# A transformer block on one core: the order of the first chunk's work, of the first-key subtraction and of the second group's normalization

## The chip, the core and the metric

One core of a Trainium2 chip runs the whole kernel. A core has TensorE (PE: matmuls and transposes, results in PSUM), VectorE (DVE), ScalarE (ACT) and GpSimd (POOL) for elementwise work, and SyncE (SP), whose queue issues all the DMAs here. Each engine runs its own queue in order; semaphores tie the queues together. The metric is the device time of one execution in microseconds (us). Before the change it is 1096.91 us, the median of 3 runs (1096.4 to 1098.2).

## The reference

Two sequences of 2048 rows with 256 channels pass a layer norm and latent attention with 16 heads, and then a layer norm and a gated FFN with 768 hidden channels; both are added to their input. Everything is fp32. Cut to what matters:

```
h    = layernorm(x)                                   # [2, 2048, 256]
kv_c = rmsnorm(h @ W_kv) * g_kv                       # 64 channels
q_c  = h @ W_q                                        # 128 channels
k    = concat(kv_c @ W_kdec, rope(h @ W_krope))       # per head 16 + 32
q    = concat(q_c @ W_qdec, rope(q_c @ W_qrope))
v    = kv_c @ W_vdec                                  # per head 16
attn = softmax(causal(q k^T / sqrt(48))) v
x    = x + attn @ W_o
h    = layernorm(x)
out  = x + (silu(h @ w_gate^T) * (h @ w_up^T)) @ w_down^T
```

## The kernel before, in words

The rows are cut into 8 chunks of 512, four for each sequence (b, g). The program has three stages, one after the other, and a fourth that is skipped with these inputs.

**Projections.** Each chunk's x is loaded (L64). `measure` takes the moments (`bn_stats` L78 and `bn_aggr` L80 on DVE, then the inverse root as an addition and a power on POOL, L69 and L70). `norm` subtracts and scales (L86, DVE). `turn` transposes the eight 128x128 blocks on PE (L97) into one PSUM tile, which ACT copies out in one instruction (L98). `compressed` makes kv (L252) and q (L255), with ACT copies, a square on ACT, a sum on DVE (L264) and an inverse root on POOL. `kv_norm` (L272, ACT) scales kv, `kv_turn` (L279) transposes it. Four rope projections, k_0, q_0, k_1, q_1 (L298 and L301), each fill a two-bank PSUM tile, which DVE reads twice to multiply it with the cosine and sine tables (L306); POOL subtracts and adds the products (L308, L309), and SP writes the result to DRAM (L311). The content projections (L319, copied by ACT L322, written at L325 and L328) and v (L335, L342) follow. The PSUM tiles come from a pool with four buffers, so a projection waits until the reader of the fourth one before it is done. The tile of cosine products has three buffers, each free when its write to DRAM has landed; the tile of sine products has two.

The loop over chunks interleaves three chunks: while chunk i is projected, chunk i + 1 is transposed and compressed, and the moments of chunk i + 2 are taken. The raw weights are loaded in front, behind the first x: w_kr, w_kv, w_q, then the first 512 columns of the tables, x of chunk 1, w_qh and the rest. `rope_columns` (L205) reorders w_kr's columns on ACT. `staged` (L168) puts raw weights into the buffers of the cosine products or of the content projections.

**Attention.** There are 32 steps (b, u, g): sequence, group of four heads, chunk of queries. A step goes through the key chunks c = 0 to g; the scores (L535, PE) go through exp (L540, ACT), on the diagonal through a mask (L547, POOL), and into the sums with v (L561, PE). No maximum is subtracted; in its place, `from_first` subtracts the sequence's first key from all keys, since that leaves the softmax as it is: on DVE, two copies of the first key (L140, only for g = 0) and two subtractions (L141) of 48x1024 for each tile of keys. Each step adds one key tile. In the projections, from the fifth chunk on, `load_first` takes from a list: the loads of the first four key tiles, of the first two query tiles, and then the four `from_first`, one entry at each of four places in a chunk. In attention, step i subtracts for step i + 3 after its fourth score block. In the last three steps the work for the FFN's groups 0 and 1 begins: `projected` (L459) and `added` (L465) for both, `measured`, `normed` and `normalized` (L499 to L501) for group 0.

**FFN.** For each of the 8 groups of 512 rows, six blocks of 128 hidden channels: gate and up on PE (L692; inputs and hidden values are split into a rounded part and a rest, `hi` and `lo`), silu on ACT (L695), the product on DVE (L699), its rest on POOL (L704). Between the blocks stand the next groups' pieces: `measured` of group i + 1 behind block 0; `finished` (the down projection of group i - 1, L720), `normed` of group i + 1, `inverted` (the reciprocal of the sums, L436), `projected` and `added` of group i + 2 behind block 1; `normalized` of group i + 1 behind block 3. `ps_o`, the transposes `tp_f` and `gu` share three PSUM buffers.

**What sets the order.** Every stage stands in a `manual_schedule` over all five engines. Where an instruction ends up in its engine's queue is decided there, and it isn't always the place that it has in the source.

Of the kernel before, what the change touches and what calls it, by code (L numbers as in the profile page):

```python
# [9 lines left out]
FP = mybir.dt.float32  # L10
# [3 lines left out]
ALU = mybir.AluOpType  # L14
# [4 lines left out]
P = 128  # L19
B, T, C = 2, 2048, 256  # L20
NH, HD, RD = 16, 16, 32
KVR, QR = 64, 128
HID = 768
CH = 512
NC = T // CH
NT = CH // P
# [14 lines left out]
def block_kernel(ctx: ExitStack, tc: tile.TileContext, x, w_kv, g_kv, w_kc, w_v, w_q, w_qh, w_kr, w_o,  # L41
                 w_gate_t, w_up_t, w_down_t, cos_t, sin_t, out):
    nc = tc.nc
# [6 lines left out]
    small = ctx.enter_context(tc.tile_pool(name="small", bufs=3))  # L50
# [11 lines left out]
    def load_x(pool, b, g, **kw):  # L62
        t = pool.tile([P, NT, C], FP, tag="x", name=f"x_{b}_{g}", **kw)
        nc.sync.dma_start(out=t, in_=x[b, g * CH:(g + 1) * CH, :].rearrange("(t p) d -> p t d", p=P))  # L64
        return t

    def inverse_sqrt(dst, src, eps):

        nc.gpsimd.tensor_scalar_add(dst, src, eps)  # L69
        nc.gpsimd.tensor_tensor(dst, dst, neg_half, ALU.pow)  # L70

    def moments(src, name):

        stats = small.tile([P, NT, 6], FP, tag="stats", name=f"stats_{name}")
        mv = small.tile([P, NT, 2], FP, tag="mv", name=f"mv_{name}")
        rstd = small.tile([P, NT], FP, tag="rstd", name=f"rstd_{name}")
        for t in range(NT):
            nc.vector.bn_stats(out=stats[:, t, :], in_=src[:, t, :])  # L78
        for t in range(NT):
            nc.vector.bn_aggr(out=mv[:, t, :], in_=stats[:, t, :])  # L80
        inverse_sqrt(rstd, mv[:, :, 1], LN_EPS)
        return mv, rstd

    def scaled(dst, src, mv, rstd):
        for t in range(NT):
            nc.vector.tensor_scalar(dst[:, t, :], src[:, t, :], mv[:, t, 0:1], rstd[:, t:t + 1],  # L86
                                    ALU.subtract, ALU.mult)

# [60 lines left out]
    with ExitStack() as actx:  # L149
# [5 lines left out]
        def two(name):  # L155
            return ps_two.tile([P, 2, CH], FP, tag="two", name=name)

        actx.enter_context(tc.manual_schedule(engines=order))
        xt = {(0, 0): load_x(prep, 0, 0, bufs=3)}

        def weight(src, shape, name, split=None):
            w = acst.tile(shape, FP, tag=name, name=name)
            nc.sync.dma_start(out=w, in_=src.rearrange("(c p) f -> p c f", p=P) if split else src)
            return w

        def staged(src, shape, name):
            w = rope.tile(shape, FP, tag="tcos" if shape[0] == P else "done", bufs=3 if shape[0] == P else 2, name=name)
            nc.sync.dma_start(out=w, in_=src)  # L168
            return w

        w_kr_raw = [staged(w_kr[d * P:(d + 1) * P, :], [P, NH * 64], f"w_kr_raw_{d}") for d in range(2)]
        w_kv_sb = weight(w_kv, [P, 2, KVR], "w_kv_sb", True)
        w_q_sb = weight(w_q, [P, 2, QR], "w_q_sb", True)

        tables = []
        for name, src in (("cos", cos_t[:RD // 2]), ("sin", sin_t[RD // 2:])):
# [23 lines left out]
        def rope_columns(w, raw):  # L200

            to = w.rearrange("p (e s h r) -> p s e h r", e=2, s=2, h=8)
            of = raw.rearrange("p (e h s r) -> p s e h r", e=2, h=8, s=4)
            for s in range(2):
                nc.scalar.copy(to[:, s], of[:, s])  # L205
# [8 lines left out]

        w_kc_sb = acst.tile([P, P], FP, tag="w_kc", name="w_kc_sb")
        w_kr_sb = acst.tile([P, 2, NH * RD], FP, tag="w_kr", name="w_kr_sb")
        for d in range(2):
            rope_columns(w_kr_sb[:, d, :], w_kr_raw[d])

        def columns():  # L220
            rope_columns(w_qr_sb, w_qh_raw)
# [129 lines left out]
        def job(i, k):  # L351
            if i < len(chunks):
                chains[i][k]()

        for k in (measure, norm, turn):
            job(0, k)
        job(1, measure)

        first_loads = ([(load_k, step) for step in steps[:NC]] + [(load_q, step) for step in steps[:AHEAD]]
                       + [(from_first, step) for step in steps[:NC]])  # L360

        def load_first(i):
            if i >= NC and first_loads:
# [3 lines left out]
        for i, one in enumerate(chunks):  # L367
            (k_0, q_0, k_1, q_1), (q_content, k_content, v) = project_jobs(*one)
            if i + 3 < len(chunks):
                xt[chunks[i + 3]] = load_x(prep, *chunks[i + 3], bufs=3)  # L370
            k_0()
            if i == 0:

                job(1, norm)
                columns()
                job(0, compressed)
                k_1()
                job(1, turn)
                job(0, kv_norm)
                job(2, measure)  # L380
                q_0()
                job(0, kv_turn)
                q_1()
                job(1, compressed)
            else:
                job(i + 2, measure)
                job(i, kv_turn)
                q_0()
                load_first(i)
                job(i + 1, turn)  # L390
                k_1()
                load_first(i)
                job(i + 1, compressed)
                q_1()
                load_first(i)
            q_content()
            job(i + 2, norm)
            k_content()
            load_first(i)
            v()  # L400
            job(i + 1, kv_norm)
            if i == 0:
                for to in kc.values():
                    nc.sync.dma_start(out=to[:, HD, :], in_=ones)
# [46 lines left out]
    x2, xns = {}, {}  # L451
# [25 lines left out]
    def taken(shape, dtype, **kw):  # L477
        return (takes[0] if takes else spare).tile(shape, dtype, **kw)
# [6 lines left out]

    def normed(b, g):

        of, xns[b, g] = xns[b, g], taken([P, NT, C], FP, tag="xn", name=f"xn_f_{b}_{g}")
        scaled(xns[b, g], x1[b, g], *of)

    def normalized(b, g):
# [12 lines left out]
    with ExitStack() as actx:  # L504
# [125 lines left out]
        with tc.manual_schedule(engines=order):  # L630

            end = len(steps) - 1
            early = {(end - 2, 1, 0): (projected, added), (end - 2, 1, 2): (measured,), (end - 1, 0, 2): (normed,),
                     (end - 1, 1, 0): (normalized,), (end - 1, 2, 0): (projected, added)}
            waiting = []
            for i, step in enumerate(steps):
                loads(i)
                by_chunk = exp_jobs(*step)
                for c, (jobs, values) in enumerate(by_chunk):
                    for k, job in enumerate(jobs):  # L640
                        job()
                        if k == 0 and waiting:
                            waiting.pop()()
                        if c == 0 and k == 3 and NC - 1 < i + NC - 1 < len(steps):
                            from_first(*steps[i + NC - 1])
                        if k in (0, 2):
                            for one in early.get((i, c, k), ()):
                                one(*groups[0 if i < len(steps) - 2 or c < 2 else 1])
                    waiting.append(values)
            waiting.pop()()  # L650

# [82 lines left out]
    with tc.manual_schedule(engines=order):  # L734
        x1[groups[2]] = load_x(fp, *groups[2], bufs=4)
        for i, one in enumerate(groups):
            parts[one] = split("hT_%d_%d" % one, [P, NF, CH])
            for f in range(NF):
                hidden(*one, f)
                if f == 0:  # L740
                    if i + 1 < len(groups):
                        measured(*groups[i + 1])
                    if 2 < i + 2 < len(groups):
                        divided(*groups[i + 2])
                    if i + 3 < len(groups):
                        packed(*groups[i + 3])
                if f == 1:
                    if i:
                        finished(*groups[i - 1])
                    if i + 1 < len(groups):  # L750
                        normed(*groups[i + 1])
                    if i + 3 < len(groups):
                        inverted(*groups[i + 3])
                    if i + 2 < len(groups):
                        projected(*groups[i + 2])
                        added(*groups[i + 2])
                if f == 3:
                    if i + 1 < len(groups):
                        normalized(*groups[i + 1])
                    if i + 3 < len(groups):  # L760
                        x1[groups[i + 3]] = load_x(fp, *groups[i + 3], bufs=4)
                if (i, f) == (len(groups) - 3, 2):
                    doubts()
                if (i, f) == (len(groups) - 3, 4):
                    flagged()
        halving.pop()()
        finished(*groups[-1])
# [194 lines left out]
```

## Time and profile before

| | us |
|---|---|
| median of 3 runs | 1096.91 |
| profiled execution, its time | 1096.71 |
| its span, first to last instruction | 1095.0 |
| PE busy | 1066.9 |
| ACT busy | 654.5 |
| DVE busy | 310.0 |
| POOL busy | 281.2 |

The span in stages, by the timeline: k_0 of chunk 0 starts at 12.44, k_0 of chunk 1 at 42.2, and every later chunk takes 18.95; the first scores start at 177.22, the FFN's first block at 922.05. Of the span, 28.1 us have no matmul or transpose running. The granted clock of PE is 0.994 of the full one on average.

The profile's page and the answers from its trace are read like this. A line of a group or of the timeline names start, duration, engine, line, operation, output<-inputs and shapes, then in brackets the idle time before it and what ended that. A line of waits names who waited, for which instruction, the sum, the count and the longest. In the row of 40 slices a digit is the busy share in tenths. Windows give the busy time of each engine in a stretch.

### The profile page before, as it was taken

How to read it: one execution, taken by the hardware profiler on the slowest of the kernel's cores; microseconds unless marked ns; L12 is line 12 of the kernel's file. 1: busy time of each engine (PE TensorE's matmuls, PEld its weight loads, DVE VectorE, ACT ScalarE, POOL GpSimd, SP SyncE). 2: the span in 40 equal slices, each digit the busy share in tenths (PEclk: the TensorE clock that was granted, in tenths of full speed). 3: DMA queues.
4: the chain of work that ended last, by engine and by line, in shares of the span. 5: the costliest groups of instructions: out<-in, count | busy, mean ns of one | idle time of the engine just before them, and what ended most of it. 6: DMA issues, size and time to landing. Idle time of an engine off the chain costs nothing.

```text
span 1095.0 us, 16796 instructions
## 1 busy us (share of the span) xinstructions
PE 1066.9 (97%) x6657; PEld 536.8 (49%) x6657; DVE 310.0 (28%) x454; ACT 654.5 (60%) x816; POOL 281.2 (26%) x377
## 2 busy tenths in 40 slices
PE   6999998999999999999999999999999999899997
PEld 3455544444433433444344344444435445788886
DVE  4677793200210210120011121003001101656552
ACT  2343344777777677777777767767776675343242
POOL 2666764111110210211121031021111001455343
PEclk9999999999999999999999999999999999999999
DMA  8556746110610421311031033122101001242201
GB/s 192 167 210 203 251 139 217 56 39 23 182 55 13 135 75 61 92 54 39 20 104 53 31 98 98 40 78 80 39 14 36 11 10 43 89 131 87 79 20 43
DMA packets 54440, 93.25 MB, mean 85 GB/s; under 512 B 9296, under 2 KB 22992, under 8 KB 54352
## 3 DMA queue, kind: packets, MB, share of 16 engines
q1 hardware_dynamic: 54352, 92.09, 27.3%
q8 instruction: 54, 0.88, 0.4%
q14 instruction: 34, 0.28, 0.1%
HBM read 49.09 MB, written 42.98 MB: 84 GB/s over the span
## 4 chain that ended last, share of the span: by engine, by line
PE 91%; DMA 4%; POOL 2%; DVE 1%; SPq 1%; issue 1%; ACT 0%; DVEq 0%; ACTq 0%; POOLq 0%
PE st L535 45%; PE acc L561 22%; PE gu L692 8%; PE d L720 4%; PE rp_k L298 3%; PE ps_o L459 3%; PE rp_q L301 2%; DMA x<-in_x_dram 2%; DMA kc<-cont_k 1%; DMA w_qh_raw<-in_w_qh_dram 1%; PE kvq L255 1%; PE kvq L252 1%; PE tp_f L499 1%; PE cp_q L319 1%; PE cp_k L319 1%
## 5 line engine op out<-in xcount | busy, mean ns | idle before, releaser
L540 ACT ACTIVATE es<-st 128x1024 f32<-128x1024 f32 (+1 forms) x576 | 513.2, 995 | 172.4 <-PE st L535 171.8
L535 PE MATMUL st<-qT,kT 48*128 48x512 f32 (+3 forms) x2560 | 496.8, 537 | 3.5 <-issue 3.0
L535 PEld LDWEIGHTS st<-qT,kT 48*128 48x128 f32 x2560 | 228.6, 186 | 251.2 <-ACT es L540 117.8
L547 POOL TENSOR_SCALAR_AFFINE_SELECT es<-es 128x256 f32<-128x256 f32 (+1 forms) x192 | 96.3, 510 | 644.2 <-ACT es L540 644.0
L561 PE MATMUL acc<-es,v_sb 128*32 128x512 f32 (+3 forms) x2560 | 250.5, 531 | 0.0
L561 PEld LDWEIGHTS acc<-es,v_sb 128*32 128x32 f32 x2560 | 74.8, 109 | 183.5 <-issue 145.4
L141 DVE TENSOR_TENSOR kT<-kT,k 48x1024 f32<-48x1024 f32 x64 | 81.8, 1279 | 155.1 <-DMA kT<-kc 108.4
L695 ACT ACTIVATE silu<-gu 128x512 f32<-128x512 f32 x48 | 28.6, 598 | 94.3 <-PE gu L692 94.3
L704 POOL TENSOR_TENSOR hT_lo<-h,hT_hi 128x512 fp32r<-128x512 f32 x48 | 61.7, 1287 | 77.3 <-ACT hT_hi L703 77.3
L298 PE MATMUL rp_k<-xln,w_kr_sb 128*128 128x512 f32 x128 | 61.1, 622 | 1.1 <-ACT xln L98 1.1
L699 DVE SCALAR_TENSOR_TENSOR h<-gu,silu 128x512 f32<-128x512 f32 x48 | 33.0, 689 | 83.8 <-ACT silu L695 58.5
L720 PE MATMUL d<-w_d,hT_lo 128*128 128x256 f32 x192 | 46.4, 283 | 0.0
L720 PE MATMUL d<-w_d,hT_hi 128*128 128x256 f32 x192 | 46.4, 283 | 0.0
L569 ACT COPY at<-acc 128x512 f32<-128x512 f32 x32 | 18.7, 585 | 38.9 <-PE acc L561 35.3
L692 PE MATMUL gu<-x_f_hi,w_g 128*128 128x512 f32 x96 | 40.0, 417 | 0.2 <-DVE h L699 0.2
L298 PEld LDWEIGHTS rp_k<-xln,w_kr_sb 128*128 128x128 f32 x128 | 24.2, 198 | 29.4 <-issue 27.6
L692 PE MATMUL gu<-x_f_lo,w_g 128*128 128x512 f32 x96 | 38.0, 396 | 0.0
L692 PE MATMUL gu<-x_f_hi,w_u 128*128 128x512 f32 x96 | 37.6, 392 | 0.0
L692 PE MATMUL gu<-x_f_lo,w_u 128*128 128x512 f32 x96 | 37.4, 390 | 0.0
L720 PEld LDWEIGHTS d<-w_d,hT_lo 128*128 128x128 f32 x192 | 36.8, 192 | 0.3
L720 PEld LDWEIGHTS d<-w_d,hT_hi 128*128 128x128 f32 x192 | 36.8, 192 | 0.3
L258 ACT COPY qc<-kvq 128x512 f32<-128x512 f32 x8 | 4.7, 586 | 44.5 <-PE kvq L255 44.5
(94 smaller groups left out, 744.1 us busy)
## 6 DMA issues: line engine op xcount, KB each, us to landing
x<-in_x_dram SPq DMA_DIRECT2D x16, 512.0 KB
kr<-tcos_k SPq DMA_DIRECT2D x16, 512.0 KB
qr<-tcos_q SPq DMA_DIRECT2D x16, 512.0 KB
kT<-kr SPq DMA_DIRECT2D x64, 128.0 KB
qT<-qr SPq DMA_DIRECT2D x64, 128.0 KB
ad<-at SPq DMA_DIRECT2D x32, 256.0 KB
vd<-v_sb SPq DMA_DIRECT2D x8, 574.0 KB
qc<-cont_q SPq DMA_DIRECT2D x8, 512.0 KB
```

The source lines that it names most:

```text
L141: nc.vector.tensor_tensor(t[rows], t[rows], k0[b, u][rows].unsqueeze(2).to_broadcast([DIM, 2, CH]), ALU.subtract)
L298: nc.tensor.matmul(ps[:, s, :], lhsT=w_kr_sb[:, d, cols], rhs=xln[b, g][:, d, :], start=(d == 0), stop=(d == 1))
L459: nc.tensor.matmul(ps[:, t * C:(t + 1) * C], lhsT=attn[b, g][:, d, t * P:(t + 1) * P], rhs=w_o_sb[:, d, :], start=(d == 0), stop=(d == 1))
L535: nc.tensor.matmul(ps[:, a, i * w:(i + 1) * w], lhsT=kT[b, u, c][rows, r, j * P:(j + 1) * P], rhs=qT[b, u, g][rows, r, off:], start=True, ...
L540: nc.scalar.activation(e[:, :, :used], ps[:, :, :used], AF.Exp, scale=SCALE)
L547: nc.gpsimd.affine_select(out=block, in_=block, compare_op=ALU.is_ge, fill=0.0, base=0, pattern=pattern, channel_multiplier=-1)
L561: nc.tensor.matmul(acc[b, u, g][r0:r0 + 32, off:], lhsT=vv[b, c][:, j, h * VW:h * VW + 32], rhs=es[kt, p][:, a], start=(kt == 0), stop=(kt ...
L692: nc.tensor.matmul(ps[:, k, :], lhsT=w[:, d, cols], rhs=x2[b, g][s][:, d, :], start=(d == 0 and s == 0), stop=(d == 1 and s == 1))
L695: nc.scalar.activation(s, ps[:, 0, :], AF.Silu, scale=WS)
L699: nc.vector.scalar_tensor_tensor(h, ps[:, 1, :], WS, s, ALU.mult, ALU.mult)
L704: nc.gpsimd.tensor_tensor(lo, h, hi.bitcast(FP), ALU.subtract)
L720: nc.tensor.matmul(ps[t], lhsT=parts[b, g][s][:, f, t * P:(t + 1) * P], rhs=w_d[:, f, :], start=(f == 0 and s == 0), stop=(f == NF - 1 and ...
```

## The change

It has four parts.

1. *First chunk.* x is loaded in two halves, with moments, normalization, transposes and copy by halves. The loads of w_kv and w_q go ahead of those of w_kr, and w_kr's columns are reordered behind the copies. 26 transposes of the identity into an otherwise unused PSUM tile go ahead of everything on PE, and four more behind the first chunk's own. `compressed` of chunk 0 goes ahead of k_0, and the moments of chunk 1 behind k_0.
2. *First-key subtraction.* `load_first` keeps only the first step's, with two empty places ahead of it; in attention, step i subtracts for step i + 1, after its second score block.
3. *Second group.* `measured` and `normed` of group 1 go from the first FFN group into the last attention step, with a buffer of another pool for the result.
4. `moments`, `scaled` and `inverse_sqrt` take the number of tiles from their input.

```diff
     def moments(src, name):
+        tiles = src.shape[1]
...
-        for t in range(NT):
+        for t in range(tiles):
             nc.vector.bn_stats(out=stats[:, t, :], in_=src[:, t, :])
...
-        xt = {(0, 0): load_x(prep, 0, 0, bufs=3)}
+        xt = {(0, 0): prep.tile([P, NT, C], FP, tag="x", bufs=3, name="x_0_0")}
+        halves = [slice(i * NT // 2, (i + 1) * NT // 2) for i in range(2)]
+        for half in halves:
+            nc.sync.dma_start(out=xt[0, 0][:, half],
+                              in_=x[0, half.start * P:half.stop * P, :].rearrange("(t p) d -> p t d", p=P))
...
-        w_kr_raw = [staged(w_kr[d * P:(d + 1) * P, :], [P, NH * 64], f"w_kr_raw_{d}") for d in range(2)]
         w_kv_sb = weight(w_kv, [P, 2, KVR], "w_kv_sb", True)
         w_q_sb = weight(w_q, [P, 2, QR], "w_q_sb", True)
+        w_kr_raw = [staged(w_kr[d * P:(d + 1) * P, :], [P, NH * 64], f"w_kr_raw_{d}") for d in range(2)]
...
-        for d in range(2):
-            rope_columns(w_kr_sb[:, d, :], w_kr_raw[d])
...
-        for k in (measure, norm, turn):
-            job(0, k)
-        job(1, measure)
+        warm = two("warm")
+        def turn_unit(times):
+            for _ in range(times):
+                nc.tensor.transpose(warm[:, 0, :P], ident, ident)
+
+        turn_unit(26)
+        xn = prep.tile([P, NT, C], FP, tag="xn", name="xn_0_0")
+        xln[0, 0] = prep.tile([P, 2, CH], FP, tag="xln", name="xln_0_0")
+        of = [moments(xt[0, 0][:, half], f"0_0_{i}") for i, half in enumerate(halves)]
+        tp = two("tp_0_0")
+        for half, one in zip(halves, of):
+            scaled(xn[:, half], xt[0, 0][:, half], *one)
+        for half in halves:
+            for t in range(half.start, half.stop):
+                for d in range(2):
+                    nc.tensor.transpose(tp[:, d, t * P:(t + 1) * P], xn[:, t, d * P:(d + 1) * P], ident)
+            cols = slice(half.start * P, half.stop * P)
+            nc.scalar.copy(xln[0, 0][:, :, cols], tp[:, :, cols])
+        turn_unit(4)
+        for d in range(2):
+            rope_columns(w_kr_sb[:, d, :], w_kr_raw[d])
...
-                       + [(from_first, step) for step in steps[:NC]])
+                       + 2 * [(lambda *step: None, steps[0])] + [(from_first, steps[0])])
...
-            k_0()
             if i == 0:
-
+                job(0, compressed)
+                k_0()
+                job(1, measure)
                 job(1, norm)
                 columns()
-                job(0, compressed)
                 k_1()
...
-                        if c == 0 and k == 3 and NC - 1 < i + NC - 1 < len(steps):
-                            from_first(*steps[i + NC - 1])
+                        if c == 0 and k == 1 and i + 1 < len(steps):
+                            from_first(*steps[i + 1])
...
-            early = {(end - 2, 1, 0): (projected, added), (end - 2, 1, 2): (measured,), (end - 1, 0, 2): (normed,),
-                     (end - 1, 1, 0): (normalized,), (end - 1, 2, 0): (projected, added)}
+            early = {(end - 2, 1, 0): ((projected, 0), (added, 0)), (end - 2, 1, 2): ((measured, 0),),
+                     (end - 1, 0, 2): ((normed, 0),), (end - 1, 1, 0): ((normalized, 0),),
+                     (end - 1, 2, 0): ((projected, 1), (added, 1)), (end, 0, 2): ((measured, 1),),
+                     (end, 1, 2): ((normed, 1),)}
...
-                    if i + 1 < len(groups):
+                    if 0 < i < len(groups) - 1:
                         measured(*groups[i + 1])
...
-                    if i + 1 < len(groups):
+                    if 0 < i < len(groups) - 1:
                         normed(*groups[i + 1])
```

More of the change, by code (lines that the diff above doesn't have):

```diff
@@ L69, in inverse_sqrt @@
         nc.gpsimd.tensor_scalar_add(dst, src, eps)
-        nc.gpsimd.tensor_tensor(dst, dst, neg_half, ALU.pow)
+        nc.gpsimd.tensor_tensor(dst, dst, neg_half[:, :dst.shape[1]], ALU.pow)
     def moments(src, name):
+        tiles = src.shape[1]
         stats = small.tile([P, NT, 6], FP, tag="stats", name=f"stats_{name}")
-        mv = small.tile([P, NT, 2], FP, tag="mv", name=f"mv_{name}")
-        rstd = small.tile([P, NT], FP, tag="rstd", name=f"rstd_{name}")
-        for t in range(NT):
+        mv = small.tile([P, NT, 2], FP, tag="mv", name=f"mv_{name}")[:, :tiles]
+        rstd = small.tile([P, NT], FP, tag="rstd", name=f"rstd_{name}")[:, :tiles]
+        for t in range(tiles):
             nc.vector.bn_stats(out=stats[:, t, :], in_=src[:, t, :])
-        for t in range(NT):
+        for t in range(tiles):
             nc.vector.bn_aggr(out=mv[:, t, :], in_=stats[:, t, :])
@@ L84, in scaled @@
     def scaled(dst, src, mv, rstd):
-        for t in range(NT):
+        for t in range(src.shape[1]):
             nc.vector.tensor_scalar(dst[:, t, :], src[:, t, :], mv[:, t, 0:1], rstd[:, t:t + 1],
@@ L385, in block_kernel @@
             else:
+                k_0()
                 job(i + 2, measure)
@@ L486, in normed @@
     def normed(b, g):
-        of, xns[b, g] = xns[b, g], taken([P, NT, C], FP, tag="xn", name=f"xn_f_{b}_{g}")
+        of = xns[b, g]
+        pool = xpool if (b, g) == groups[1] else takes[0] if takes else spare
+        xns[b, g] = pool.tile([P, NT, C], FP, tag="xn", name=f"xn_f_{b}_{g}")
         scaled(xns[b, g], x1[b, g], *of)
@@ L643, in block_kernel @@
                             waiting.pop()()
-                        if c == 0 and k == 3 and NC - 1 < i + NC - 1 < len(steps):
-                            from_first(*steps[i + NC - 1])
+                        if c == 0 and k == 1 and i + 1 < len(steps):
+                            from_first(*steps[i + 1])
                         if k in (0, 2):
-                            for one in early.get((i, c, k), ()):
-                                one(*groups[0 if i < len(steps) - 2 or c < 2 else 1])
+                            for one, g in early.get((i, c, k), ()):
+                                one(*groups[g])
                     waiting.append(values)
```

## The prediction

> **What bounds the kernel now.** I read the page first, then TensorE's waits, then the timeline around each.
>
> ```profile
> PE 1066.9 (97%) x6657; PEld 536.8 (49%) x6657; DVE 310.0 (28%) x454; ACT 654.5 (60%) x816; POOL 281.2 (26%) x377
> ...
> PE   6999998999999999999999999999999999899997
> ...
> PE 91%; DMA 4%; POOL 2%; DVE 1%; SPq 1%; issue 1%; ACT 0%; DVEq 0%; ACTq 0%; POOLq 0%
> ```
>
> PE is busy for 97% of the span and is 91% of the chain that ended last, so only PE's gaps and its clock can be won. 1095.0 - 1066.9 = 28.1 us of gaps. The waits say where they are:
>
> ```profile
> PE tp L97 <- DVE xn L86: 9.0, 1, 9.0
> PE st L535 <- issue: 3.0, 1, 3.0
> PE tp_f L499 <- DVE x L465: 2.8, 1, 2.8
> PE cp_k L319 <- DVE tsin_q L306: 2.7, 1, 2.7
> PE ktp L279 <- ACT kvn L272: 1.6, 1, 1.6
> ```
>
> One start, one end of the projections (ktp, st), one start of the FFN (tp_f), and cp_k in chunk 0. The change has one edit for each. The rows that price them, from four windows of the timeline:
>
> ```profile
> 9.04 2.29 PE L97 MATMUL tp<-ident,xn 128*128 128x128 f32 x8 [9.04 <-DVE xn L86]
> 12.44 6.38 PE L298 MATMUL rp_k<-xln,w_kr_sb 128*128 128x512 f32 x8 [1.10 <-ACT xln L98]
> ```
> ```profile
> 34.79 1.40 DVE L78 BATCH_NORM_STATS2 stats<-x 128x6 f32<-128x256 f32 x4 [6.64 <-DMA x<-in_x_dram]
> ```
> ```profile
> 149.99 3.70 DVE L141 TENSOR_TENSOR kT<-kT,k 48x1024 f32<-48x1024 f32 x2
> 155.99 3.42 DVE L141 TENSOR_TENSOR kT<-kT,k 48x1024 f32<-48x1024 f32 x2
> 174.77 1.22 DVE L306 TENSOR_TENSOR tcos_q<-rp_q,cos 128x1024 f32<-128x1024 f32 x1 [3.56 <-DMA kr<-tcos_k]
> ```
> ```profile
> 167.77 1.03 SPq L311 DMA_DIRECT2D kr<-tcos_k  x1
> ```
> ```profile
> 930.85 3.37 DVE L86 TENSOR_SCALAR xn_f<-x,mv_f,rstd_f 128x256 f32<-128x256 f32 x4 [0.91 <-POOL rstd_f L70]
> 934.15 0.54 DVE L436 RECIPROCAL rec<-all_sums 128x64 f32<-128x64 f32 x1
> 934.61 1.15 DVE L465 TENSOR_TENSOR x<-ps_o,x 128x1024 f32<-128x1024 f32 x1
> ```
>
> The reader is to see: the first transposes take 0.29 us each, where chunk 1's eight take 1.04 in all; k_0's eight matmuls take 6.38, where later ones take 3.60: a cold clock until about 17.85. A pair of subtractions costs 3.4 to 3.7 us where POOL works beside it, against 1.22 each alone. The granted clock falls for one stretch of 3.41 us after each of the three later gaps (0.93 in the windows 25 to 50, 175 to 200 and 925 to 950); each such stretch costs about 1.7.
>
> **Start.** *Removed:* half of the wait for x, and the cold clock. *Added:* 30 transposes of the identity, one DMA, three small DVE/POOL steps. Before: x at 5.41, statistics 1.41, aggregates 0.36, rstd 1.48 with its gaps, normalizing 1.38, transposes 2.29, copy 1.01, k_0 at 12.44. After, from the second half (landing 5.4 to 5.9): 0.71 + 0.18 + 1.48 + 0.69 = 8.5 to 9.0; its last transposes 0.3 to 0.6; its half of the copy about 0.55: compressed from about 10.0. Beside warm rows (18.65 to 22.16, so 3.5): 13.5. The w_kr columns, 4 x 0.71 = 2.84 on ACT behind the copies, end by 12.9 and are covered. k_0 then 3.6, to 17.1; its two DVE products (1.22 each) end at about 19.3; k_1 ends at about 20.6. But chunk 1's statistics now stand behind k_0's products on DVE, and its rstd behind POOL's 2 x 1.27: 19.3 + about 6 = 25.2 for its transposes (25.59 before). PE idles 4.6 there, the clock falls once, and cp_q ends at about 37 to 38.7 (36.17 before). That costs nothing, since cp_k waits for tsin_q, which stands behind the statistics of chunk 2, whose x lands at 34.79. Its DMA stands on SP behind the sine table, which waits for w_qh; that order is unchanged. So cp_k still starts near 38.86, but warm: 2.08 becomes 1.13, and v and the rest follow sooner. Chunk 1's k_0 at 40.9 instead of 42.2. I take **-1.0** (-1.4 to +0.3). From there to chunk 6 PE has no gap, and the gain is carried.
>
> **A rule against it.** All this needs transposes of the identity to open the clock. The row: at 936.0 to 939.4 PE's time was about 37% transposes and 63% matmuls, and the clock rose at the end of it; a window only 67% busy (11.02 to 14.43, transposes and matmuls) did not raise it. That leans to transposes counting. The Trainium skill, "TensorE: Matmul & The Clock Gate", Part 4 (PE-mode transpose), says the opposite: a transpose does not count as PE work, and the full clock does not engage for it. By the rule, compressed runs at half speed: with cold tp rows it starts near 10.3 to 12.4 and takes up to 7, k_0's products end at about 24.5, chunk 1's transposes come at 30, cp_k at 42.3, k_0 at 44.3 to 45: **+2 to +3** instead of -1.0. I take the row (7 in 10): it is this chip, though a mixed window.
>
> **End of the projections.** The diff says that three of the four steps' subtractions leave the projections for attention. The built order says otherwise: on DVE all eight subtractions and both copies now stand in chunks 6 and 7. Five subtractions and two copies stand between q_0 and k_1 of chunk 6 (there were two and none), two behind k_1's products (as before), the last behind q_1's. Those of steps 0 and 1 leave chunk 5, where they had made DVE late: k_0's products of chunk 6 started at 145.45, PE done at 141.4. So up to 4 us of lateness goes, and 3 subtractions (1.22 to 1.85 each, alone or beside POOL) and 2 copies (up to 1.32) come: 3.7 + 1.0 to 5.6 + 2.6. Net +0.7 to +4 at k_1. Waiting behind: k_1's products, hence k_0 of chunk 7 on PE (it needs the PSUM buffer), the last kv sums, hence ktp (which waited 1.57 already), q_1's products and POOL's sums behind them. On SP qr moves from 164.73 and with it qc, kc and then kr of chunk 7, which landed 7.0 us after its issue at 167.77. The last tsin_q, and with it the first st, waits for that landing. Stepping the queues through, in the times of before, kr is issued at 169.4 to 171.7, st starts at 178.8 to 181.2 instead of 177.22. The longer gap can cost a second half of a cold stretch (0 to 1.7). I take 2.6 + 0.7 = **+3.3** (+1 to +6). Nothing hides it: attention is PE-bound from its first matmul.
>
> The later subtractions, one step ahead, have the time: a tile of new keys is needed only in a step's last chunk, or, for a first chunk, after a whole four-chunk step; DVE is busy 2.44 of 25 us there (200 to 225). 0.
>
> **FFN.** Chunk 2's statistics and normalizing (1.39 + 0.36, then 3.37 beside POOL) leave DVE's queue ahead of the reciprocal and the addition that frees the PSUM buffer of tp_f. They go into the last attention step, where DVE is idle (0.00 busy in 900 to 925). Then the reciprocal is next, which waits for all_sums (its transfers end near 932), and the addition ends at about 933.6 instead of 935.76; PE is done with gu at 932.9. The wait of 2.75 becomes 0.7 and the cold stretch (1.7) need not come: 2.05 + 1.7, **-3.6** (-1.5 to -4.5). The first group took 25.6 us where later ones take 21.06, which bounds it.
>
> **Sum:** -1.0 + 3.3 - 3.6 = -1.3 against the profiled execution (span 1095.0, time 1096.71): 1095.4. The median of the runs is 1096.91, 0.2 above it. No change is within 0.2%, some 2.2 us.
>
> **Rivals.**
> 1. *Transposes don't open the clock.* For it the rule, and that no stretch of transposes alone is in the trace; against it the row. +2.7 + 3.3 - 3.6 = +2.4: 1099.1. Chance 0.23.
> 2. *The end of the projections costs nothing.* For it: DVE idles 1.04, 1.08 and 3.56 us behind the place, and kr's 7 us are a backlog which may drain while DVE is late. Against it: kr's issue is what the last products wait for. -1.0 - 0.5 - 3.6: 1091.6. Chance 0.15. (Were the three steps' work really in attention, the waits of ktp and st and the cold stretch would go, 1.6 + 3.0 + 1.7, and it would be near 1087; the built order excludes it.)
> 3. *DVE and POOL take turns through all five subtractions*, the slower side: at 1.85 each and with POOL's sums at 2.25 instead of 1.27, kr goes out 5 us later, st's gap reaches 8, one whole further stretch is cold: +6.7, in sum +2.1, with a smaller gain at the FFN +4. It makes the change slower than before once st starts more than 4.6 us late with its clock. For it the two pairs above; against it that POOL has little to do between q_0's sums and k_1's. 1100. Chance 0.22.
> 4. *Forecast*, 0.40: 1095.4, its own range 1092.5 to 1098.5.
>
> **Chances.** Faster by over 0.2%: 0.14 of the forecast's 0.40, nearly all of rival 2: 0.30. Slower: half or more of rivals 1 and 3, 0.03 of the forecast: 0.31. Same: 0.39. The range, 1090.5 to 1101.5, takes rival 2 and the middles of 1 and 3, and leaves out their outer halves.
>
> **What would show it.** Start: compressed near 10 and at 3.5 us, the granted clock full before 10; else rival 1. tp of chunk 1 near 25 with about 4.6 idle; cp_k near 38.9. End: kr of chunk 7 issued near 170.5 less the start's gain, st waiting 5 us or more. FFN: tp_f's wait under 1 us and no 0.93 in its window. Wrong would make it: x of chunk 2 landing sooner or later than 34.8, or kr landing much faster than 7 us.

## The result and the profile after

The changed kernel takes 1102.03 us in the median (1100.98 to 1104.02, 5 runs), the kernel before 1096.96 (1096.4 to 1098.2, 5 runs). The ratio is 1.0049, with a 95% interval of 1.0034 to 1.0063: slower by half a per cent, where the forecast was 1095.4 and its range ended at 1101.5. The profiled execution took 1100.98 us with a span of 1099.3 and a mean granted clock of 0.990 (0.994 before).

The page's first part for the changed kernel:

```profile
PE 1073.1 (98%) x6687; PEld 541.2 (49%) x6687; DVE 308.4 (28%) x454; ACT 654.6 (60%) x817; POOL 280.4 (26%) x379
```

PE's gaps shrank (1099.3 - 1073.1 = 26.2 us, 28.1 before), but PE is busy 6.2 us longer. The 30 new transposes are 5.4 of these (4.79 and 0.60 below). They lie in what was a gap; elsewhere new gaps opened and matmuls ran at half clock. Below, *cold* means that the granted clock is at 0.50 of the full one, and a *cold stretch* runs from a fall of the clock to its next rise. PE's waits (engine, line, for what: sum, count, longest):

```profile
PE st L562 <- issue: 5.0, 1, 5.0
PE tp L98 <- DVE xn L87: 3.5, 1, 3.5
PE ktp L283 <- ACT kvn L276: 2.6, 1, 2.6
PE cp_k L323 <- DVE tsin_q L310: 2.5, 1, 2.5
PE tp_f L526 <- DVE x L489: 2.0, 1, 2.0
...
PE acc L588 <- POOL es L574: 0.7, 1, 0.7
```

The long wait of tp at the start is gone, and a new one of 3.5 stands before chunk 1's transposes. st and ktp wait longer, cp_k nearly as long as before, tp_f 0.8 less, and acc waits where it had not. The same places in the timelines of both profiled executions:

| start of | before | after | difference | added since the row above |
|---|---|---|---|---|
| k_0, chunk 1 | 42.20 | 41.87 | -0.33 | -0.33 |
| first scores st | 177.22 | 179.90 | +2.68 | +3.01 |
| copy of the first step's acc | 187.75 | 191.66 | +3.91 | +1.23 |
| copy of step 28's acc | 829.87 | 834.04 | +4.17 | +0.26 |
| copy of step 29's acc | 851.30 | 856.36 | +5.06 | +0.89 |
| copy of step 31's acc | 922.19 | 927.25 | +5.06 | 0 |
| last silu | 1082.31 | 1086.65 | +4.34 | -0.72 |

**Start.** PE's timeline (start, duration), then one line of DVE's, then cp_q and cp_k of the kernel before:

```profile
1.42 4.79 PE L363 MATMUL warm<-ident 128*128 128x128 f32 x26 [1.42 <-POOL ident masks.py:199]
...
8.69 1.90 PE L256 MATMUL kvq<-w_kv_sb,xln 128*128 128x64 f32 x16
10.42 1.94 PE L259 MATMUL kvq<-xln,w_q_sb 128*128 128x512 f32 x4
12.19 7.03 PE L302 MATMUL rp_k<-xln,w_kr_sb 128*128 128x512 f32 x16
22.69 2.30 PE L98 MATMUL tp<-ident,xn 128*128 128x128 f32 x8 [3.47 <-DVE xn L87]
...
34.21 1.88 PE L323 MATMUL cp_q<-qc,w_qc_sb 128*128 128x512 f32 x4
38.63 1.60 PE L323 MATMUL cp_k<-kvc,w_kc_sb 64*128 64x512 f32 x4 [2.54 <-DVE tsin_q L310]
```
```profile
34.56 1.41 DVE L79 BATCH_NORM_STATS2 stats<-x 128x6 f32<-128x256 f32 x4 [8.69 <-DMA x<-in_x_dram]
```
```profile
34.29 1.88 PE L319 MATMUL cp_q<-qc,w_qc_sb 128*128 128x512 f32 x4
38.86 2.08 PE L319 MATMUL cp_k<-kvc,w_kc_sb 64*128 64x512 f32 x4 [2.69 <-DVE tsin_q L306]
```

compressed, k_0 and k_1 are done at 19.2 and at full clock, 6.5 us sooner than before. Then all of it is given back. The clock falls in the 3.5 us gap and stays down for 6.8 us (chunk 1's transposes take 2.30, not 1.04), so cp_q is done at 36.1 as before (36.17). DVE waits 8.69 us for chunk 2's x. cp_k starts about where it had started, and the clock falls again while it runs (1.60 us, where it takes 1.13 warm and took 2.08 before).

**End of the projections.** DVE, POOL, SP and PE of the changed kernel, then PE of the kernel before:

```profile
149.72 4.86 DVE L142 TENSOR_TENSOR kT<-kT,k 48x1024 f32<-48x1024 f32 x4
154.50 1.21 DVE L310 TENSOR_TENSOR tcos_k<-rp_k,cos 128x1024 f32<-128x1024 f32 x1
...
157.20 4.28 DVE L142 TENSOR_TENSOR kT<-kT,k 48x1024 f32<-48x1024 f32 x2
...
177.44 1.23 DVE L310 TENSOR_TENSOR tcos_q<-rp_q,cos 128x1024 f32<-128x1024 f32 x1 [4.95 <-DMA kr<-tcos_k]
```
```profile
163.82 2.31 POOL L312 TENSOR_TENSOR tcos_q<-tcos_q,tsin_q 128x512 f32<-128x512 f32 x1 [1.13 <-DVE tsin_q L310]
```
```profile
170.43 0.99 SPq L315 DMA_DIRECT2D kr<-tcos_k  x1
```
```profile
179.90 9.40 PE L562 MATMUL st<-qT,kT 48*128 48x512 f32 x40 [5.01 <-issue]
```
```profile
177.22 8.17 PE L535 MATMUL st<-qT,kT 48*128 48x512 f32 x40 [3.05 <-issue]
```

Five subtractions stand before k_1's products (the first, at 146.29, is not in these rows), but those start only 0.8 later than before (153.71). The rest of the delay arises behind them. Two more subtractions take 4.28 (3.42 before), so q_1's products are done at 163.74 (162.12 before); POOL's two sums behind those take 3.54 together (2.50 before), with the last subtraction beside the first of them. So kr goes out 2.7 later than before. It lands 7.0 after that, as it did; st starts 2.7 later, and its first 40 matmuls take 9.40 instead of 8.17.

### The profile page after: what moved, and what is told of

Read it like the earlier page. It is cut to its first block, busy times and chain, and to the rows that moved or that the text cites. A ratio compares the mean times of both kernels' runs of the same rounds, so it can differ in the third digit from the quotient of the medians.

```text
span 1099.3 us, 16856 instructions
## 1 busy us (share of the span) xinstructions
PE 1073.1 (98%) x6687; PEld 541.2 (49%) x6687; DVE 308.4 (28%) x454; ACT 654.6 (60%) x817; POOL 280.4 (26%) x379
## 4 chain that ended last, share of the span: by engine, by line
PE 91%; DMA 3%; DVE 2%; POOL 1%; issue 1%; SPq 1%; ACT 0%; DVEq 0%; ACTq 0%; POOLq 0%
PE st L562 44%; PE acc L588 22%; PE gu L721 8%; PE d L749 4%; PE rp_k L302 4%; PE ps_o L483 3%; PE rp_q L305 2%; DMA x<-in_x_dram 1%; DMA w_qh_raw<-in_w_qh_dram 1%; PE kvq L259 1%; PE kvq L256 1%; PE cp_q L323 1%; PE tp_f L526 1%; DMA kc<-cont_k 1%; PE cp_k L323 1%
## 5 line engine op out<-in xcount | busy, mean ns | idle before, releaser
L302 PE MATMUL rp_k<-xln,w_kr_sb 128*128 128x512 f32 x128 | 58.4, 601 | 0.0
L460 DVE RECIPROCAL rec<-all_sums 128x64 f32<-128x64 f32 x8 | 4.4, 549 | 162.9 <-DMA all_sums<-ad 162.9
L489 DVE TENSOR_TENSOR x<-ps_o,x 128x1024 f32<-128x1024 f32 x8 | 9.7, 1217 | 99.5 <-PE ps_o L483 99.5
```

The costliest lines, as they stand in the source:

```text
L302: nc.tensor.matmul(ps[:, s, :], lhsT=w_kr_sb[:, d, cols], rhs=xln[b, g][:, d, :], start=(d == 0), stop=(d == 1))
```

## Experiments

Each kernel was compared with the kernel before on the same chip, where that took 1094.8 to 1095.3; the expectations with whole times still reckon from 1097.0, so they are read as differences to it. The differences are of medians. The ratios, each with its 95% interval, are the recorded ones; they are not the quotients of these medians and lie up to 0.0011 (1.2 us) off them. The single executions of one kernel spread by several us, so a profile shows a mechanism and the ratio its size.

The expectations call their theories by letters. A: the place of the subtractions in DVE's queue makes the loss. B: kr lands late because of the DMA backlog, whenever it is issued. C: the start or the FFN part has a share in the loss. D: chunk 2's x holds cp_k up and swallows the start's gain. E: the tables hold things up next. F: the landing of all_sums ends tp_f's wait. G: a pair of subtractions makes POOL late, and with it a mask.

**The parts alone.** Only the new start, only the subtraction part, only the FFN part of the change, on the kernel before:

> The kernel before with only the new start (x in halves, weights reordered, turning, compressed first). Theory D (x of chunk 2 gates cp_k, and with one DMA more ahead of it in the ring it is issued 0.5 to 2 us later; a second cold stretch comes from the idle time before chunk 1's transposes): 2 to 3.5 us slower than before. The prediction's own step: 1.0 faster.

Measured: 1097.32 against 1095.25, ratio 1.0016 (1.0006 to 1.0027): 2.1 slower, as D says. cp_k starts at 38.73 in its profile, and the clock falls again at 39.2. That execution itself was one of the quicker ones (1094.25).

> The kernel before with only the subtraction part of the change. Theory A: 1101.5 to 1102.5, first st near 180. Rival C: 1099 or less.

Measured: 1099.59 against 1095.3, 1.0037 (1.0024 to 1.0050): 4.3 slower, a little less than the 4.5 to 5.5 of A; st starts at 179.76, as A said. Most of the loss is this part's.

> The kernel before with only the FFN part. Theory F (all_sums' landing takes over the wait of tp_f, so only 0.5 to 1 us of 2.75 goes, and the cold stretch goes in some executions only): 0.7 to 2 us faster. The prediction's own step: 3.6 faster.

Measured: 1094.19 against 1095.25, 0.9988 (0.9980 to 0.9995): 1.1 faster, as F says. The parts add up: by the medians 2.1 + 4.3 - 1.1 = 5.3, where the whole change is 5.1; by the ratios 0.41%, where it is 0.49%, which is within the intervals.

**The subtractions taken back.** In the changed kernel, start and FFN parts kept:

```diff
-                       + 2 * [(lambda *step: None, steps[0])] + [(from_first, steps[0])])
+                       + [(from_first, step) for step in steps[:NC]])
...
-                        if c == 0 and k == 1 and i + 1 < len(steps):
-                            from_first(*steps[i + 1])
+                        if c == 0 and k == 3 and NC - 1 < i + NC - 1 < len(steps):
+                            from_first(*steps[i + NC - 1])
```

> The changed kernel with the four subtractions back in chunks 5 and 6 and, in attention, three steps ahead; start and FFN parts stay. Theory A (the subtractions' place costs 4 at the end of the projections and 0.9 at step 29): 1096 to 1097, first st near 177.0, no wait of acc for GpSimd's es at step 29. Rival C (part of the loss comes from the new start or from the FFN part): 1099 or more.

Measured: 1097.94 against 1095.3, 1.0026 (1.0014 to 1.0038). That is 2.6 slower than before: half of the loss goes, and acc no longer waits for es. But 2.6 stay, where A expected none: C is right that another part has a share, and by the kernels with one part that is the start. In its profile chunk 2's x lands at 36.19, and cp_k waits 4.2.

**The subtractions really moved.** Those of steps 1 to 3 written behind the last projection, in the projections' own schedule:

```diff
+        for step in steps[1:NC]:
+            from_first(*step)
...
-                        if c == 0 and k == 1 and i + 1 < len(steps):
+                        if c == 0 and k == 1 and NC <= i + 1 < len(steps):
                             from_first(*steps[i + 1])
```

> The changed kernel, with the subtractions of steps 1 to 3 written behind the last projection, so that on VectorE they stand behind the last rope products (only step 0's stay in chunk 6). Theory A (VectorE's queue decides): k_1's products of chunk 6 start near 149.7 instead of 154.5, the kr write of chunk 7 goes out near 165 instead of 170.4, ktp's wait of 2.6 goes, the first st starts before 176 with little cold clock: 1092 to 1096. Rival B (the write's landing is bound by the DMA backlog, not by its issue): kr lands near 177 whatever its issue, st still waits 3 us or more: 1097 to 1099.

Measured: 1093.3 against 1095.3, 0.9978 (0.9969 to 0.9988). 2 us faster than before, where the change is 5.1 slower. SP and PE:

```profile
165.73 0.33 SPq L315 DMA_DIRECT2D kr<-tcos_k  x1
```
```profile
172.88 3.35 PE L565 MATMUL st<-qT,kT 48*128 48x512 f32 x16 [1.21 <-ACT v_sb L346]
```

kr goes out 4.7 sooner than in the changed kernel and lands by 170.3, after 4.5 us and not 7; st waits 1.2 for the copy of v instead of 5.0 for the last products, and there is no cold stretch there. The landing follows the issue: A, not B.

**The transposes of the identity left out.**

```diff
-        turn_unit(26)
...
-        turn_unit(4)
```

> The changed kernel without the 30 transposes of the identity. Theory A (transposes open the clock, but cp_k's wait for chunk 2's x hides most of it): compressed and k_0 run cold, chunk 1's transposes near 26 instead of 22.7, cp_q ends near 39 instead of 36.1, cp_k at 39 to 40: 1102 to 1103.5. The rule (transposes don't count for the clock): compressed and k_0 take as long as with them, 1102.0, and the clock rises at the same time.

Measured: 1100.16 against 1095.3, 1.0053 (1.0035 to 1.0070), which can't be told from the change's 1.0049. PE:

```profile
9.32 3.52 PE L256 MATMUL kvq<-w_kv_sb,xln 128*128 128x64 f32 x16
12.63 3.58 PE L259 MATMUL kvq<-xln,w_q_sb 128*128 128x512 f32 x4
16.04 7.03 PE L302 MATMUL rp_k<-xln,w_kr_sb 128*128 128x512 f32 x16
```

The same 20 matmuls of compressed take 3.52 and 3.58 instead of 1.90 and 1.94. The first change of the clock in the trace's own list is a rise: at 5.0 us in the changed kernel, when PE had run nothing but transposes of the identity, and at 15.9 here. So turning the identity opens the clock here, and the rule falls. In these two profiles cp_k's wait for chunk 2's x takes most of the gain back: cp_q ends at 40.05 instead of 36.09, but cp_k starts at 39.98 instead of 38.63. That this is the whole reason is not shown; the two kernels without the wait, below, gain little from the transposes either.

**Chunk 2's x ahead of the tables.**

```diff
+        xt[0, 2] = load_x(prep, 0, 2, bufs=3)
         for _, others, src in tables:
             nc.sync.dma_start(out=others, in_=src[:, :, CH:])
-        xt[0, 2] = load_x(prep, 0, 2, bufs=3)
```

> The changed kernel with the load of chunk 2's x ahead of the rest of the two tables on SyncE. Theory D (x of chunk 2 is the gate that swallows the new start's gain): x lands before 30, cp_k of chunk 0 follows cp_q near 36 without a wait, k_0 of chunk 1 near 38.5 instead of 41.9, and one of the two cold stretches goes: 4 to 5 us less than the changed kernel, 0 to 1 over the kernel before. Rival E (the tables, now later, become the gate): k_0's products of chunk 1 wait for the cosine table, k_0 of chunk 2 no sooner than with the change: no gain.

Measured: 1096.15 against 1094.76, 1.0014 (1.0003 to 1.0026): 3.8 less than the change by the ratios. PE, then DVE:

```profile
35.31 1.13 PE L323 MATMUL cp_k<-kvc,w_kc_sb 64*128 64x512 f32 x4
...
39.41 5.40 PE L302 MATMUL rp_k<-xln,w_kr_sb 128*128 128x512 f32 x8 [2.11 <-DVE tsin_q L310]
```
```profile
37.00 1.23 DVE L310 TENSOR_TENSOR tcos_q<-rp_q,cos 128x1024 f32<-128x1024 f32 x1 [6.55 <-DMA kr<-tcos_k]
```

x is there before 26.15, and cp_k follows cp_q without a wait. E has a part in it: the tables are now issued behind that load, q_1's products wait 6.55 for the landing of kr's first write, and chunk 1's k_0 starts at 39.41, not 38.5. The second cold stretch, which D expected to go, came there (40.8 to 44.2).

> As the one before, without the 30 transposes of the identity. Theory D: with the gate gone, the warm clock of the first chunk shows in the time: 2 to 4 us slower than the one with transposes. If the transposes are worth nothing even then: the same time.

Measured: 1097.11 against 1094.76, 1.0020 (1.0012 to 1.0028): 1.0 more than with the transposes by the medians, and the intervals overlap. Chunk 1's k_0 starts 1.9 later (41.30) in the profile, but the clock then does not fall a second time.

**The sums' load earlier.** Group 3's softmax sums are loaded in the last attention step (`summed` is the last part of `packed`, which loads them):

```diff
-                     (end - 1, 2, 0): ((projected, 1), (added, 1)), (end, 0, 2): ((measured, 1),),
+                     (end - 1, 2, 0): ((projected, 1), (added, 1)), (end, 0, 0): ((summed, 3),), (end, 0, 2): ((measured, 1),),
...
+        if (b, g) not in parts_of:
+            summed(b, g)
```

> The changed kernel with the load of group 3's softmax sums issued in the last attention step instead of behind x and attn at the FFN's start. Theory F (all_sums' landing ends the wait of tp_f): the reciprocal runs right behind the second product, the addition at once behind ps_o, tp_f's wait of 2.0 and the cold stretch behind it go: 3 to 4 us less than the changed kernel. Rival: another transfer or the products are late next: under 1 us less.

Measured: 1096.61 against 1094.76, 1.0006 (0.9995 to 1.0016): 4.7 less than the change by the ratios, 3.2 by the medians. The reciprocal in the changed kernel, and then in this one:

```profile
938.48 0.55 DVE L460 RECIPROCAL rec<-all_sums 128x64 f32<-128x64 f32 x1 [4.83 <-DMA all_sums<-ad]
```
```profile
933.24 0.54 DVE L465 RECIPROCAL rec<-all_sums 128x64 f32<-128x64 f32 x1
934.87 1.23 DVE L494 TENSOR_TENSOR x<-ps_o,x 128x1024 f32<-128x1024 f32 x1 [1.08 <-DMA x<-in_x_dram]
```

tp_f's wait is gone, and so is the cold stretch behind it.

**All three mends together.**

> The changed kernel with all three: the subtractions of steps 1 to 3 behind the last projection, chunk 2's x ahead of the tables, group 3's sums in the last attention step. If the three are separate: 7 + 4.5 + 3.5 = 15 less than the changed kernel, 9 to 10 less than the kernel before, 1085 to 1087 where before is 1095.3. If the end of the projections takes back the start's gain: 1089 or more.

Measured: 1086.69 against 1094.76, 0.9920 (0.9905 to 0.9934): 8 us faster than before, 15 expected below the change and 14 found (1.0049 - 0.9920). PE's waits, all of them over 1 us and the next:

```profile
PE tp L98 <- DVE xn L87: 3.5, 1, 3.5
PE warm L363 <- POOL ident masks.py:199: 1.4, 1, 1.4
PE acc L596 <- POOL es L582: 1.2, 2, 0.7
PE st L570 <- ACT v_sb L346: 1.2, 1, 1.2
PE tp L375 <- ACT xln L377: 0.7, 1, 0.7
```

> The kernel with all three mends, without the 30 transposes of the identity. With nothing behind the start that takes its gain back, compressed and k_0 cold (15.8 instead of 12.0 for k_0's start) should cost their whole 3 to 4 us. If the transposes are worth nothing: no difference from the one with them (0.992 of before).

Measured: 1087.01 against 1095.25, 0.9921 (0.9908 to 0.9934), the same as with them. The two profiled executions differ by 2.7 us (1083.79 with, 1086.46 without), the medians of five runs by 0.3. With the transposes two of the five executions, 1086.69 and 1088.22, were granted a clock of 0.994 and the others 0.996 or 0.997, as all five without them; but the third slow one (1087.38) had 0.996. So what takes the 3.7 us of k_0's earlier start (11.99, 15.67 without) back in the other executions stays open.

**The last step's subtraction ahead of group 0's moments.**

```diff
-                        if c == 0 and k == 1 and NC <= i + 1 < len(steps):
+                        if c == 0 and k == 1 and NC <= i + 1 < end:
                             from_first(*steps[i + 1])
+                        if (i, c, k) == (end - 2, 0, 1):
+                            from_first(*steps[end])
```

> The kernel with all three mends, and the last step's subtraction two steps ahead, before the moments of group 0 instead of behind them. Theory G (the pair of subtractions holds up GpSimd's rstd, which stands before the diagonal masks in GpSimd's queue): no wait of acc for es at step 29, 0.7 to 1 us faster than with the three alone. Rival (the rstd itself, 1.3 us, is enough to make the mask late): the wait stays, same time.

Measured: 1085.23 against 1095.25, 0.9911 (0.9897 to 0.9925). The step from step 28's copy of acc to step 29's is 21.41, as before the change (21.43), and 22.32 in the changed kernel; in this one acc does not wait for es at step 29. DVE and POOL in the changed kernel, then POOL here:

```profile
851.24 2.76 DVE L142 TENSOR_TENSOR kT<-kT,k 48x1024 f32<-48x1024 f32 x2
...
852.89 1.19 POOL L69 TENSOR_SCALAR rstd_f<-mv_f 128x4 f32<-128x4 f32 x1
854.16 1.04 POOL L70 TENSOR_TENSOR rstd_f<-rstd_f,neg_half 128x4 f32<-128x4 f32 x1
855.17 0.64 POOL L574 TENSOR_SCALAR_AFFINE_SELECT es<-es 128x512 f32<-128x512 f32 x1
```
```profile
841.37 0.23 POOL L69 TENSOR_SCALAR rstd_f<-mv_f 128x4 f32<-128x4 f32 x1
841.68 1.04 POOL L70 TENSOR_TENSOR rstd_f<-rstd_f,neg_half 128x4 f32<-128x4 f32 x1
842.69 0.64 POOL L582 TENSOR_SCALAR_AFFINE_SELECT es<-es 128x512 f32<-128x512 f32 x1
```

Beside the two subtractions the small POOL instruction takes 1.19 instead of 0.23, and the last mask behind it is late. G is shown by the trace; in the time alone the two kernels' intervals overlap. This is the fastest kernel of the study, 10 us below the kernel before.

## Why the prediction was wrong, step by step

- **Start, -1.0: wrong in sign; 2.1 slower alone (0.7 to 3.0 by the interval).** The gate was named (cp_k near 38.86 because of chunk 2's x; 38.63 measured), and what comes ahead of it was even faster than forecast (compressed at 8.69, not 10.0; chunk 1's transposes at 22.69, not 25.2). What failed is "cp_k still starts near 38.86, but warm", and "the clock falls once". cp_q was done at 36.1, not 37 to 38.7, so the gap before cp_k stayed about as long as before, and a second cold stretch came: in all five profiles with the new start, its transposes and the late x. With the old start it came in one of three, and that one was the profile that the forecast reckoned from: chunk 1's k_0 started there at 42.2, but at 40.7 in the two others, where the five start it at 41.9 to 44.0. "That order is unchanged" was true of SP's queue but not of its time: chunk 2's x was issued at 18.4 to 20.0 and landed at 34.6 to 36.2 in the six profiles with the new start and the late load, and at 17.3 to 17.9 and 34.4 to 34.8 in the three with the old. That the DMA added by the halves causes this was not tried alone.
- **The rule.** The row was the right choice: transposes count here. What they are worth in time is another matter: in the three pairs of kernels with and without them the medians put it at 1.0 us or less.
- **End of the projections, +3.3: right in mechanism and nearly in size.** kr at 170.43 (forecast 169.4 to 171.7), landing 7.0 later, st at 179.90 (178.8 to 181.2), a longer cold stretch: +4.2 in the profile from chunk 1's k_0 to the first copy of acc.
- **Later subtractions, 0: mis-sized.** DVE has the time, as forecast, but the POOL instructions beside it don't: +0.9 at step 29. The two terms were put at 3.3 together; the profiles show 5.1 and the part alone 4.3 (2.6 to 5.5).
- **FFN, -3.6: mis-sized, -1.1 alone.** The step that failed is "its transfers end near 932". all_sums is issued behind x and two attn loads, at 933.02, and the reciprocal waited for it until 938.48, 11.4 behind the first block (927.12), which in the times of before is 933.4. The addition then ended at 940.1, PE still waited 2.0, and the clock fell. The 1.7 for the cold stretch was mis-sized too: of three profiles with the old order only the one forecast from has that stretch, of seven with the new order and the late load three have it. With the sums loaded earlier the stretch from the first block to the last silu takes 155.7 in the profile, where it was 160.3 before and 158.6 and 159.0 in the two profiles with the old order and no cold stretch. (The terms 2.05 and 1.7 make 3.75, not 3.6.)

The rivals: the first fell. The second fell as the change was built; the kernel with the three steps' work behind the projections shows that its remark on the built order was the point. (The aside to it, 1.6 + 3.0 + 1.7 off, comes to 1085.8 and not to 1087.) The third had the right side, but st came only 2.7 late. The miss of 6.6 comes from three terms, each off the same way: start 3.1, subtractions 1.0, FFN 2.5.

## What to carry to other kernels

A chain that is made faster gains only up to the next transfer that it meets: look up what lands last, and move that load first. Where the built order decides, read it for every engine, and put work that is meant to run later where the schedule can't draw it forward. A gap that is shortened but not closed can still bring its cold stretch. And a cold stretch in one profile of the kernel before is not in all its executions: its removal can't be counted whole.

## What the runs showed of the hardware

Two windows of the changed kernel (stretch, length, busy time and count of PE, its weight loads, DVE, ACT and POOL, granted clock, DMA share, GB/s), PE busy throughout the second, at half the clock:

```profile
22.00:24.00 2.00, 1.31 (x5) 0.89 (x6) 1.84 (x5) 0.00 (x0) 0.79 (x3) 0.52 1.12 173
...
40.00:42.00 2.00, 2.00 (x11) 1.31 (x7) 2.00 (x4) 1.04 (x2) 2.00 (x2) 0.50 0.04 14
```

By such windows of 0.4 us or by the trace's own list of clock changes, in the profiled executions (the first rise, from the cold start, is left out):

| kernel | clock falls and rises, 12 to 52 us |
|---|---|
| before | 38.3 to 41.8 |
| FFN part alone, subtraction part alone | none |
| changed | 22.1 to 28.9, 39.2 to 42.6 |
| new start alone | 22.1 to 29.0, 39.2 to 42.6 |
| changed, subtractions as before | 22.1 to 28.9, 39.2 to 46.0 |
| changed, subtractions really moved | 22.0 to 28.8, 39.1 to 42.5 |
| changed, sums' load earlier | 24.4 to 27.8, 38.1 to 44.9 |
| changed, chunk 2's x ahead | 23.7 to 27.1, 40.8 to 44.2 |
| the same without the transposes | 27.1 to 30.5 |
| changed, without the transposes | 26.2 to 33.0 |
| three mends | 21.6 to 28.4 |
| three mends, without the transposes | 26.5 to 29.9 |

In these traces a stretch lasts 3.4 us or twice that. A gap of nearly one length brings it in one execution and not in another: before cp_k, 2.7 us did in the kernel before, 3.0 didn't with the FFN part alone. This goes with most of the spread of the executions: over the 57 runs of the kernel before on one chip, a line through time and mean granted clock falls by 6.6 us for each 0.01 of clock (correlation -0.79, so part of the spread has another source).
